# Last batch's FFN in rounds of four row groups, with Gelu taken straight from four PSUM banks

## The chip, the cores and the metric

The kernel runs on one core of a Trainium2 chip. The metric is the device time of one execution in microseconds; a kernel's time is the median of its runs. Before the change it is 4330.48 us, the median of three runs of 4320.04, 4330.48 and 4338.9 us.

## The reference

The whole computation is a two-layer network over 4 images of 384 channels and 32 x 32 positions. Layer 0 is a selective scan followed by a mixture of four experts with two chosen for each token. Layer 1 is an attention with eight heads followed by an FFN whose weights are Kronecker products. The change lies in the last of these, which is, cut to what matters:

```python
def _L1_ffn_ref(x, c_fc_1, c_fc_2, c_proj_1, c_proj_2):
    w_fc = jnp.kron(c_fc_1, c_fc_2)
    w_proj = jnp.kron(c_proj_1, c_proj_2)
    h = x @ w_fc.T
    h = jax.nn.gelu(h, approximate=False)
    out = h @ w_proj.T
    return out
...
x = x + _L1_conv_ref(_ln_c(x), L1_conv_w_qkv, L1_conv_w_out, L1_conv_b_out)
t = _to_tokens(x)
t = t + _L1_ffn_ref(_ln_t(t), L1_ffn_c_fc_1, L1_ffn_c_fc_2, L1_ffn_c_proj_1, L1_ffn_c_proj_2)
```

`w_fc` is the product of 1536 x 32 and 1 x 12 factors, `w_proj` of 32 x 1536 and 12 x 1. Because of this, the first matrix can be applied in two steps: 384 channels are reduced to 32 values (here called z), and these are multiplied by a 32 x 1536 matrix. The second matrix likewise: 1536 hidden values are reduced to 32, which are spread to 384 channels.

## The kernel before

The kernel is one program in which the four batches overlap. `scan_layer` does the selective scan of all batches, one after the other. While it scans a batch, the tail (experts, attention, FFN) of the batch before is laid beside it by a scheduler that runs a timeline of its own when the program is built and fixes the order of instructions on each engine. The tail of the last batch has no scan beside it. It runs in a wider set of buffers: `WIDE` for SBUF and, from its attention on, `WIDE_BANKS` for PSUM, which has 6 banks with the tag "p" and 2 with the tag "o", where `NARROW_BANKS` has 3 and 1.

The FFN is in `last_layers`. For each half `i` of the positions (512 of 1024 columns) a first part forms x2, the input of the FFN (L1149 to L1155, `o_ps`), its mean and variance by matmuls with ones (L1160 `x_mean`, L1177 `x_var`, with squares on ACT, L1168), and z: a matmul `z_ps` (L1171), scaled by the inverse root of the variance, which ACT works out as an Ln and an Exp (`inverse_root`, L152 and L153) and DVE multiplies in (L1180). z holds the same 32 values four times, once in each group of 32 partitions.

The second part is a loop over the two halves, with the 1536 hidden values in 12 chunks of 128, `f` = 0 to 11:

- `hidden(i, at)` makes six chunks (`ng = 6`). For each, a matmul `h_ps` (L1193) multiplies 32 rows of z by a piece of `fc1`. Chunk `f` uses the row group `f % 4` of TensorE, so that matmuls of different chunks can run in different rows of the array. They go two at a time: two banks are filled, two copies on ACT (L1199) bring them to the SBUF tile `hs`, and the next pair's first matmul is made to wait for the first copy of the pair before. Then one activation applies Gelu to the whole `hs`, 3072 columns (L1202), in place.
- Then six matmuls `f_acc` (L1210) reduce `hs` to 32 values. Chunk `f` writes to the column group `f % 4`, so these too can run beside one another, in different columns of the array. A first product and the later ones of the same column group accumulate in one bank with the tag "o".
- After two such rounds DVE copies the accumulated bank (`fy`, L1215), three matmuls `fo_ps` (L1218) spread it to 384 channels (adding up the four column groups), DVE adds x2 (L1220), and the result is stored (L1221).

Gelu and Exp need different function tables on ACT. The builder of the program puts a load of a table (ACT_TABLE_LOAD) before any activation whose function is not in the active one. `exp_again` (L145 to L148) puts a load of the table that holds both Ln and Exp directly behind a given activation, with high priority, so that the exponentials of the scan and of the attention never find a table that lacks them:

```python
self.exp_again(nc.scalar.activation(hs, hs, AF.Gelu).ins)
```

`hs` has the tag "k12", of which the wide room has three buffers. x2 holds one of them until the end, so `hs` alternates between two.

Of the kernel before, what the change touches and what calls it, by code (L numbers as in the profile page):

```python
# [11 lines left out]
AF = mybir.ActivationFunctionType  # L12
# [5 lines left out]
P = 128  # L18
# [5 lines left out]
HF = 512  # L24
# [34 lines left out]
KR = 32  # L59
# [29 lines left out]
WIDE_BANKS = {"o": 2, "p": 6}  # L89
# [26 lines left out]
class Body:  # L116
# [993 lines left out]
    def last_layers(self, b, att, room):  # L1110
# [4 lines left out]
        nc, a = self.nc, self.a  # L1115
        nq = P // KR
# [11 lines left out]
        fc1 = wc[:, 0, :].rearrange("p (q m) -> p q m", m=P)  # L1128
# [9 lines left out]
        zs = []  # L1138
        for i in range(NH):
# [4 lines left out]
            for c in range(DC):  # L1144
                ps = room.bank("p", "o_ps")
# [4 lines left out]
                for j in range(HF // P):  # L1150
                    nc.tensor.matmul(  # L1151
                        ps[:, j * P : (j + 1) * P], part[j // 2][:, j % 2, chunk], self.ident,
                        start=False, stop=(j == HF // P - 1),
# [16 lines left out]
            for c in range(DC):  # L1170
                nc.tensor.matmul(  # L1171
                    zp, wz[:, c * P : (c + 1) * P], x2[:, c, halves(i)],
                    start=(c == 0), stop=(c == DC - 1),
# [7 lines left out]
            zs.append(z)  # L1181


        ng = 6

        def hidden(i, at):
            hs = room.tile([P, ng, HF], "k12", "hs")
            early = None
            for f in range(at, at + ng, 2):
                banks = [room.bank("p", "h_ps") for _ in range(2)]  # L1190
                for o, ps in enumerate(banks):
                    rows = slice((f + o) % nq * KR, ((f + o) % nq + 1) * KR)
                    ins = nc.tensor.matmul(  # L1193
                        ps, fc1[rows, (f + o) // nq, :], zs[i][rows, :], start=True, stop=True
                    ).ins
                    if o == 0 and early is not None:
                        self.depend(ins, early)
                done = [
                    nc.scalar.copy(hs[:, f - at + o, :], ps).ins for o, ps in enumerate(banks)  # L1199
                ]  # L1200
                early = done[0]
            self.exp_again(nc.scalar.activation(hs, hs, AF.Gelu).ins)  # L1202
            return hs

        for i in range(NH):
            out = room.bank("o", "f_acc")
            for at in range(0, FC, ng):
                hs = hidden(i, at)
                for f in range(at, at + ng):
                    nc.tensor.matmul(  # L1210
                        out[f % nq * KR : (f % nq + 1) * KR, :], pj1[:, f, :], hs[:, f - at, :],
                        start=(f < nq), stop=(f >= FC - nq),
                    )
            y = room.tile([P, HF], "k4", "fy")
            nc.vector.tensor_copy(y, out)  # L1215
            for c in range(DC):
                ps = room.bank("p", "fo_ps")
                nc.tensor.matmul(ps, pj2[:, c * P : (c + 1) * P], y, start=True, stop=True)  # L1218
                o = room.tile([P, HF], "k4", "out")
                nc.vector.tensor_add(o, ps, x2[:, c, halves(i)])  # L1220
                nc.sync.dma_start(out=a["out"][b][c * P : (c + 1) * P, halves(i)], in_=o)  # L1221
# [236 lines left out]
```

## Time and profile before

The profiled execution took 4328.09 us; its span, from the first to the last instruction, is 4326.3 us.

| what | value |
|---|---|
| median of three runs | 4330.48 us |
| profiled execution, and its span | 4328.09 us, 4326.3 us |
| mean granted clock of TensorE | 0.868 of full speed |
| busy over the whole span: PE, DVE, ACT, POOL | 77%, 66%, 58%, 70% |
| last batch's FFN, 4256 to 4320 us: ACT copies (L1199) | 24, 588 ns each |
| ACT Gelu (L1202) | 4, 2762 ns each |
| ACT table loads (L1202 and L148) | 8, 1283 ns each |
| PE idle ahead of f_acc (L1210), waiting for Gelu | 20.9 us |
| ACT idle ahead of its copies, waiting for h_ps | 18.3 us |
| after the last add: flag, branch, stores landing | 4320.1 to 4326.3 us |

How to read it: the busy shares of the whole span say little about this change, since each stage has its own limits. The last 120 us of the span belong to the last batch's layer 1 alone, with PE, ACT and DVE only. In matmul rows, "128*32" is rows by columns of the array that the weights take; a matmul in fp32 is recorded as two passes, so x4 is two matmuls. A line number can be that of a helper: L152 and L153 are the Ln and Exp of `inverse_root`, L148 is the load of `exp_again`.

### The profile page before, as it was taken

The numbers are of one execution on the slowest core, as the hardware profiler recorded it, in microseconds if no ns is written. First come the engines' busy times: TensorE is split into PE (matmuls) and PEld (weight loads), VectorE is DVE, ScalarE is ACT, GpSimd is POOL, SyncE is SP. The second block draws the span as 40 slices with busy tenths as digits, with TensorE's granted clock in tenths as the row PEclk, the third lists the DMA queues.
The fourth block names the chain that finished last, engine by engine and source line by source line (L and its number), as shares of the span: only waits on it lengthen the run. The fifth ranks groups of instructions, "written<-read, shape, count | busy, mean of one in ns | idle before, by whom it ended". The sixth has DMA issues, their size and how long they took to land. (4 is left out here: it accounts for less than half of the span.)

```text
span 4326.3 us, 45583 instructions
## 1 busy us (share of the span) xinstructions
PE 3343.5 (77%) x13244; PEld 1557.7 (36%) x13244; DVE 2860.4 (66%) x4200; ACT 2517.2 (58%) x4484; POOL 3021.3 (70%) x1471
## 2 busy tenths in 40 slices
PE   6445454388997895779996887669998889999896
PEld 2111111155552222235553222216555235566322
DVE  5999997878786868678886778777887720000101
ACT  5555555456665776566764777476666654344354
POOL 5999997798898968889898689778899810000100
PEclk8666666599998997879998999769998999999997
DMA  5444564567895535558789335547889343345100
GB/s 141 129 120 129 138 166 113 178 198 228 232 278 142 138 113 167 156 157 241 220 235 269 112 100 149 160 121 210 242 227 297 99 157 105 109 141 203 50 26 19
DMA packets 410322, 693.69 MB, mean 160 GB/s; under 512 B 51024, under 2 KB 209616, under 8 KB 410064
## 3 DMA queue, kind: packets, MB, share of 16 engines
q1 hardware_dynamic: 400752, 664.29, 52.9%
q0 software_dynamic: 8192, 25.17, 1.8%
q8 instruction: 106, 1.74, 0.2%
q14 instruction: 152, 1.25, 0.1%
q10 hardware_dynamic: 1120, 1.25, 0.1%
HBM read 569.00 MB, written 121.50 MB: 160 GB/s over the span
## 5 line engine op out<-in xcount | busy, mean ns | idle before, releaser
L440 POOL TENSOR_TENSOR bx<-dtr,bcs 128x1024 f32<-128x1024 f32 x768 | 1794.6, 2364 | 202.1 <-PE acc L475 109.4
L449 ACT ACTIVATE da<-dtr,nega 128x512 f32<-128x512 f32 x1536 | 1045.1, 690 | 940.0 <-DVE bx L461 574.9
L468 POOL TENSOR_TENSOR bx<-bx,bcs 128x1024 f32<-128x1024 f32 x384 | 906.0, 2364 | 154.1 <-DVE carry L465 70.6
L475 PE MATMUL acc<-bx,sel 128*32 128x512 f32 x3072 | 501.5, 709 | 319.1 <-POOL bx L468 270.7
L927 PE MATMUL h_ps<-xc,w 128*128 128x256 f32 (+1 forms) x3168 | 664.8, 365 | 64.5 <-DMA w<-in_w 20.2
L942 PE MATMUL y_ps<-w,hs 128*128 128x384 f32 x1824 | 643.2, 505 | 46.7 <-ACT hs L935 39.8
L927 PEld LDWEIGHTS h_ps<-xc,w 128*128 128x128 f32 x3168 | 549.9, 197 | 236.8 <-issue 95.0
L454 DVE TENSOR_TENSOR_SCAN bx<-da,carry,bx 128x512 f32<-128x512 f32 x384 | 473.4, 1270 | 117.3 <-POOL bx L440 62.5
L454 DVE TENSOR_TENSOR_SCAN bx<-da,bx 128x512 f32<-128x512 f32 x384 | 452.4, 1211 | 120.1 <-ACT da L449 66.3
L454 DVE TENSOR_TENSOR_SCAN da<-da,carry,bx 128x512 f32<-128x512 f32 x384 | 476.5, 1273 | 80.0 <-ACT da L449 67.9
L461 DVE TENSOR_TENSOR bx<-da,bcs 128x512 f32<-128x512 f32 x768 | 510.5, 680 | 3.7
L454 DVE TENSOR_TENSOR_SCAN da<-da,bx 128x512 f32<-128x512 f32 x384 | 455.0, 1219 | 55.8 <-ACT da L449 44.9
L942 PEld LDWEIGHTS y_ps<-w,hs 128*128 128x128 f32 x1824 | 349.9, 196 | 334.7 <-issue 74.3
L1057 ACT ACTIVATE ex<-s_ps 128x512 f32<-128x512 f32 x512 | 299.9, 590 | 159.7 <-PE s_ps L1051 157.9
L1051 PE MATMUL s_ps<-w 64*128 64x512 f32 x1024 | 306.2, 657 | 56.7 <-ACT ex L1057 55.1
L963 POOL TENSOR_TENSOR diag<-ident,g_weight 128x1024 f32<-128x1024 f32 x8 | 15.1, 1901 | 453.9 <-PE xc_ps L910 440.7
L932 ACT ACTIVATE hs<-h_ps,bb 128x256 f32<-128x256 f32 (+1 forms) x528 | 201.1, 440 | 181.9 <-PE h_ps L927 178.1
L1097 PE MATMUL o_acc<-ex,vt 128*64 128x512 f32 x1024 | 285.9, 633 | 20.0 <-ACT ex L1057 15.7
L475 PEld LDWEIGHTS acc<-bx,sel 128*32 128x32 f32 x3072 | 76.4, 117 | 617.6 <-POOL bx L468 378.3
L946 DVE TENSOR_TENSOR y<-y_ps,bb 128x384 f32<-128x384 f32 x76 | 41.6, 548 | 236.6 <-PE y_ps L942 236.5
L365 PE MATMUL dt_ps<-xd,wdt 108*128 108x512 f32 x192 | 125.5, 741 | 85.5 <-ACT mag L404 53.3
L1051 PEld LDWEIGHTS s_ps<-w 64*128 64x128 f32 x1024 | 82.3, 188 | 255.3 <-ACT ex L1057 211.8
(217 smaller groups left out, 3605.0 us busy)
## 6 DMA issues: line engine op xcount, KB each, us to landing
w<-in_w SPq DMA_DIRECT2D x352, 576.0 KB
dtr<-dd SPq DMA_DIRECT2D x1536, 128.0 KB
bcs<-both SPq DMA_DIRECT2D x512, 128.0 KB
dd<-one_e SPq DMA_DIRECT2D x96, 256.0 KB
dd<-mag SPq DMA_DIRECT2D x96, 256.0 KB
rows<-zero SPq DMA_DIRECT2D x76, 192.0 KB
xt<-x SPq DMA_DIRECT2D x32, 384.0 KB
xs<-rows SPq DMA_DIRECT2D x32, 384.0 KB
```

The costliest lines, as they stand in the source:

```text
L440: pool = nc.gpsimd.tensor_mul(bx, dtr[q][1], bc[:, 0].unsqueeze(1).to_broadcast([P, 2, HF])).ins
L449: nc.scalar.activation(da, dtr[q][0][:, j, :], AF.Exp, scale=nega[:, col : col + 1])
L454: nc.vector.tensor_tensor_scan(run(h), run(da), run(bx[:, j, :]), 0.0 if first else hold, ALU.mult, ALU.add,)
L461: dve = nc.vector.tensor_mul(bx[:, j, :], h, cg).ins
L468: pool = nc.gpsimd.tensor_mul(bx, bx, cg.unsqueeze(1).to_broadcast([P, 2, HF])).ins
L475: nc.tensor.matmul(acc[lo : lo + DB, :], sel, out[q][:, j, :], start=(g == 0), stop=(g == NG - 1),)
L927: nc.tensor.matmul(ps[:, r, :], w1[(f + r) // wf][:, c, (f + r) % wf * P : ((f + r) % wf + 1) * P], xc[:, c, :], start=(c == 0), stop=(c = ...
L932: nc.scalar.activation(hs[:, f + r, :], ps[:, r, :], AF.Identity, bias=bb[:, f + r : f + r + 1])
L942: nc.tensor.matmul(out[:, :D], hs[:, f, t * P : (t + 1) * P], w2[f // wf][:, f % wf, :], start=(f == 0), stop=(f == FC - 1),)
L1051: ins = nc.tensor.matmul(ps, w[rows, j * P : (j + 1) * P], w[rows, halves(i)], start=True, stop=True).ins
L1057: done.append(nc.scalar.activation(ex[:, o, :], ps, AF.Exp, scale=HD**-0.5, accum_out=sums[:, t, 2 * j + o, i : i + 1],).ins)
L1097: ins = nc.tensor.matmul(out[cols, :], made[t][1][:, j, cols], ex[:, o, :], start=(j == 0), stop=(j == MB - 1),).ins
```

## The change

In the FFN of the batch that runs with `WIDE_BANKS`, that is the last one, a round is four chunks in place of six, one for each row group. A new function `quickly` takes four banks, issues the four matmuls `h_ps` one after the other with no dependency between them, and then applies Gelu to each bank on its way from PSUM to `hs`: four activations of 512 columns, in place of copies and one Gelu of 3072. It doesn't call `exp_again`. The loop over the rounds and the f_acc matmuls are as before, with `ng` of 4, so each half has three rounds. The other batches, and the exact second layer that isn't run with these inputs, keep the rounds of six.

```diff
-        ng = 6
+        alone = room.banks is WIDE_BANKS
+        ng = nq if alone else 6
+
+        def quickly(i, at):
+
+            hs = room.tile([P, ng, HF], "k12", "hs")
+            banks = [room.bank("p", "h_ps") for _ in range(nq)]
+            for o, ps in enumerate(banks):
+                rows = slice(o * KR, (o + 1) * KR)
+                nc.tensor.matmul(
+                    ps, fc1[rows, at // nq, :], zs[i][rows, :], start=True, stop=True
+                )
+            for o, ps in enumerate(banks):
+                nc.scalar.activation(hs[:, o, :], ps, AF.Gelu)
+            return hs
 
         def hidden(i, at):
+            if alone:
+                return quickly(i, at)
             hs = room.tile([P, ng, HF], "k12", "hs")
             early = None
             for f in range(at, at + ng, 2):
```

In the changed kernel the lines behind the new ones move by 16, except that `h_ps` of the last batch is L1193, its Gelu L1197, f_acc L1226, fy L1231, fo_ps L1234 and the last add L1236.

## The prediction

> **What bounds the kernel now.** I read the page first: section 2 gives POOL, ACT and DVE the first nine tenths, and section 4's chain has PE alone in the last tenth. The change touches one branch of one function, so I went to that place: the chain of waits from 4180 us on, then stretches of 3.41 us, then PE's timeline.
>
> The chain in the last batch's FFN (start, us, what):
>
> ```profile
> 4261.29 1.18 PE h_ps L1193 x8
> 4262.47 1.05 ACT hs L1199 x2
> 4263.54 1.28 ACT L1202
> 4264.84 2.77 ACT hs L1202
> 4267.65 3.47 PE f_acc L1210 x12
> ...
> 4283.68 4.92 PE fo_ps L1218 x6
> 4288.60 1.11 PE h_ps L1193 x4
> ...
> 4319.36 0.69 DVE out L1220
> ```
>
> PE and ACT take turns: matmul, copy, table load, Gelu of 3072 columns, matmul. A round of six row groups starts its f_acc 11.56 us after the one before (4267.65, 4279.21), and there are four rounds. From the end of x_var (next matmul at 4259.31 in the timeline) to the end of the last add (4320.05) the FFN takes 60.7 us, 1.4% of the span. Nothing runs beside it.
>
> The second bound is PE's clock. Stretches of 3.41 us, laid on the moments at which the granted clock changes (span; busy us of PE, PEld, DVE, ACT, POOL; clock; DMA share; GB/s):
>
> ```profile
> 2840.65:2844.07 3.42, 1.82 (x8) 0.29 (x8) 3.35 (x6) 2.98 (x6) 2.95 (x2) 1.00 0.30 100
> 2844.07:2847.48 3.41, 0.00 (x0) 0.00 (x0) 3.39 (x6) 3.38 (x5) 2.85 (x2) 1.00 0.48 156
> 2847.48:2850.89 3.41, 1.15 (x8) 0.39 (x10) 0.94 (x3) 3.39 (x2) 3.41 (x3) 0.50 0.00 0
> ```
>
> ```profile
> 4270.86:4274.28 3.42, 2.45 (x10) 0.60 (x8) 0.00 (x0) 1.35 (x3) 0.00 (x0) 1.00 0.00 0
> 4274.28:4277.69 3.41, 0.00 (x0) 0.00 (x0) 0.00 (x0) 3.38 (x4) 0.00 (x0) 0.50 0.00 0
> 4281.10:4284.52 3.42, 2.57 (x9) 0.50 (x2) 0.69 (x1) 0.00 (x0) 0.00 (x0) 0.50 0.00 0
> 4284.52:4287.93 3.41, 3.41 (x5) 1.35 (x4) 1.12 (x2) 0.00 (x0) 0.00 (x0) 0.50 0.16 62
> 4287.93:4291.34 3.41, 2.74 (x10) 0.60 (x8) 0.96 (x2) 1.07 (x2) 0.00 (x0) 1.00 0.43 169
> ```
>
> A stretch's work decides the clock of the next. The one from 2840.65 keeps full clock with PE busy 1.82 us; the one from 4270.86 loses it with 2.45 us. The former holds column-tiled matmuls that use all 128 rows (acc), the latter mostly h_ps of 32 rows. So I weigh streaming time by the share of rows in use, counting matmuls on different columns together once: the former has 1.65/3.41 = 0.48, the latter (0.19 + 4 x 0.43 x 1/2)/3.41 = 0.31. Over all 929 full-clock stretches of the trace, 0.38 separates those that keep the clock from those that lose it but for 7; over the 333 at half clock, 0.74 separates those that regain it but for 9. Weighing by rows times columns leaves 13 and 15 misfits.
>
> PE's timeline where two tilings alternate, at full clock and then at half:
>
> ```profile
> 2836.63 1.13 PE L1193 MATMUL h_ps<-z,wc 32*128 32x512 f32 x4
> 2837.69 1.05 PE L475 MATMUL acc<-bx,sel 128*32 128x512 f32 x2
> 2838.66 1.13 PE L1193 MATMUL h_ps<-z,wc 32*128 32x512 f32 x4
> ```
>
> ```profile
> 1849.57 1.94 PE L475 MATMUL acc<-bx,sel 128*32 128x512 f32 x8
> 1851.43 2.08 PE L1193 MATMUL h_ps<-z,wc 32*128 32x512 f32 x4
> 1853.44 1.94 PE L475 MATMUL acc<-bx,sel 128*32 128x512 f32 x8
> ```
>
> From start to start an h_ps turn costs 1.06 us and an acc turn 0.98; at half clock 2.01 and 1.86. The turn costs that whether it holds one matmul or four (acc x2 is one matmul in two passes, x8 is four).
>
> [...] four h_ps on four row groups took 1.14 us, no more than two; a change of mode costs about 0.1 to 0.2 us over two passes of 0.43. [...] Here the load is 1283 ns and the next activation starts 0.02 us later, [...].
>
> **The change, part by part.** The instruction order of the changed kernel is the same on POOL, SP and DVE up to the flag (and in all earlier batches).
>
> Removed: 24 copies of 0.59 us, four Gelus of 2.76, eight table loads of 1.28. On the path they were 11.56 us a round less the f_acc.
>
> Added on ACT: 24 Gelus from PSUM and four table loads. The loads don't vanish: the scheduler puts Ln and Exp of the second half's z between the first four Gelus and the rest, so ACT runs load, 4 Gelus, load, Ln, load, Exp, load, 20 Gelus. A Gelu 128x512 from PSUM isn't in this trace; nearest is Exp from PSUM (L1057, 590 ns); pitch between 0.48 (the pair of copies, 1.07 us) and 0.58 (three L1155, 1.84 us). I take 0.60 and 0.52. First load 4256.42 to 4257.70, four Gelus to 4259.92, load, Ln 0.69, load, Exp 0.63, load: 4265.1. z's product on DVE (0.69) is ready at 4264.55.
>
> Moved on PE: the order is h0-3, x_var, then f0 h4 f1 h5 f2 h6 f3 [h7 h8 h9] f4 h10 f5 h11 [f6-9] [f10 f11], fo; in the second half h0-3, h4 h5, then f and h in turn, f0 to h11, [f6-9] [f10 f11], fo. So f and h, which before ran two or four at once, now mostly run alone: that is the price. First half from 4259.31: 6 f turns x 0.98 + 6 h turns x 1.06 = 12.2, the last six f 0.12 + 4 x 0.43 = 1.83: 4273.4. Then 0.2 to the end of the accumulation, fy 0.70, and fo at 4274.35. That needs full clock: an f and an h turn weigh (0.85 + 0.85/4)/2.03 = 0.52, above 0.38, so it holds. fo at full clock is 6 x 0.43 + 0.1 to 0.2 = 2.75 (4.92 before): 4277.1. Second half: h0-3 and h4 h5 2.0, 12.2, 1.83 = 16.1: 4293.2; accumulation, fy, three fo and the last add 4.7: 4297.9. Before: 4320.05. **Gain 22.2 us.**
>
> What hides ACT: the fifth Gelu ends at 4265.7 and f4's turn comes at 4267.4; h9 needs z at 4266.4, there at 4264.55. In the second half Gelu needs 0.52 for a PE pair of 2.03. [...] Reused hs buffers wait for f turns already past. The banks of h4 and h5 in the second half wait for the adds of fo, 0.7 us after fo, as now. On the other side, turns that overlapped would gain up to 10 us.
>
> The profiled execution is 4328.09 us, with span 4326.3; the median shown is 4330.48, 2.4 above. Before's tail also depends on where the 3.41 us grid falls: moving it over the same schedule made before's end 0 to 6 us later (mean 3), while the changed one, at full clock throughout, does not move. I take 24.5 off the median: **4306 us**.
>
> **The rivals.**
> - Area counts, not rows: lone f and h turns weigh a quarter, the clock falls at about 4264 and again in the second half. Then first half: 4281.8; fo at half clock to 4287.5; second half seven turns at full clock and seven at half: end 4318.4, gain 1.7, **4329 us**. For it: the misfits are few either way. Against: the stretches shown. If only the first half falls, 4319.
> - Slower: full clock is lost before f0 of each half and can't come back, as (1.71 + 0.43)/3.87 = 0.55 is under 0.74. Then 6 x 1.86 + 6 x 2.01 + 3.4 = 26.6 a half; end 4328.7, **8.6 later, 4339 us**. It decides if a stretch under 0.38 lies at the start of a half; the h0-5 there run four at once and follow dense matmuls, which speaks against it.
> - More: f and h overlap or turns are shorter, ACT's Gelus bind: about 8 us less, **4298 us**.
> - "Not reloaded" is not what happens (four loads remain); costed above.
>
> **How the numbers follow.** Forecast 0.72 (own range 4299 to 4314, since the runs before spread over 19 us), area 0.12, slower 0.06, more 0.10. 0.5% is 21.7 us, a line at 4308.8 and 4352 for what can be told from no change here: the forecast lies just past it, so I put 0.60 of its 0.72 beyond. Faster 0.60 + 0.10 = 0.70; slower by over 0.5% only if half clock meets the upper end of the spread of the runs, 0.03; same 0.27. Range 4294 to 4322: [...].
>
> **What would show it.** PEclk 1.00 from 4256 us to the end; f_acc alone per turn at 0.98, h_ps 1.06; four table loads after 4256 us; the last add about 22 us earlier; ACT waiting for h_ps, not PE for Gelu. Wrong if the clock reads 0.50 within the f and h turns, if turns take 1.9 us, or if PE waits for Gelu over 4 us.

## The result, and the profile after

The changed kernel takes 4311.09 us (median of 16 runs, 4303.55 to 4330.8) against 4330.12 us of the kernel before (16 runs on the same chip, 4317.05 to 4345.93). The ratio is 0.9957, with a 95% interval of 0.9944 to 0.9971: 19 us less, between 12.6 and 24.2. The forecast was 4306 us, in a range of 4294 to 4322.

The single runs of one kernel spread over 27 to 29 us, so a stage of 60 us is better measured inside the traces. The measure used below is **the tail: from the start of the first x_var matmul of the last batch's second half to the end of the last add**. It was 4255.28 to 4320.05 before, 64.77 us, and is 4258.63 to 4301.93 now, 43.30 us: 21.5 us less. Each tail below comes from one trace; the kernel before, traced twice, gave 64.77 and 64.67 us.

The two profiled executions differ by less, 4328.09 - 4310.15 = 17.9 us. The part ahead of the tail, in which the order of instructions is the same, took 3.35 us longer in the profile after, and what follows the last add 0.2 us longer.

The chain of waits of the changed kernel (start, us, what):

```profile
4258.63 1.12 PE x_var L1177 x2
...
4262.74 0.98 PE f_acc L1226 x2
4263.71 1.05 PE h_ps L1193 x2
4264.76 0.98 PE f_acc L1226 x2
...
4274.91 1.89 PE f_acc L1226 x12
...
4277.63 2.84 PE fo_ps L1234 x6
4280.47 1.91 PE h_ps L1193 x10
4282.38 0.04 issue
4282.41 1.12 PE h_ps L1193 x2
4283.53 0.98 PE f_acc L1226 x2
...
4301.24 0.69 DVE out L1236
```

ACT has left the chain. PE alone carries it: one f_acc, one h_ps, one f_acc, at 0.98 and 1.05 us a turn, and fo_ps at full clock in 2.84 us where it took 4.92. The first fo_ps starts 19.00 us after the tail's start.

ACT's timeline of the changed kernel (start, us, line, operation; in brackets the idle time ahead and what ended it):

```profile
4263.16 1.28 ACT L152 ACT_TABLE_LOAD   x1
4264.46 0.69 ACT L152 ACTIVATE z<-x_var,eps 128x512 f32<-128x512 f32 x1
4265.16 1.28 ACT L153 ACT_TABLE_LOAD   x1
4266.45 0.63 ACT L153 ACTIVATE z<-z 128x512 f32<-128x512 f32 x1
4267.10 1.28 ACT L1197 ACT_TABLE_LOAD   x1
4268.40 1.58 ACT L1197 ACTIVATE hs<-h_ps 128x512 f32<-128x512 f32 x3
...
4274.95 0.60 ACT L1197 ACTIVATE hs<-h_ps 128x512 f32<-128x512 f32 x1 [1.43 <-PE h_ps L1193]
```

Three of the four loads are seen here, and each is followed within 0.02 us of its end by the next activation. A lone Gelu from a bank takes 0.60 us, and ACT waits for h_ps ahead of it.

A stretch of 3.41 us in the second half (busy us of PE, PEld, DVE, ACT, POOL; clock; DMA share; GB/s):

```profile
4284.45:4287.86 3.41, 3.41 (x8) 0.85 (x8) 0.00 (x0) 1.04 (x3) 0.00 (x0) 1.00 0.00 0
```

The clock is 1.00 in it, and in every stretch of the tail.

One thing wasn't foreseen. DVE's timeline between the halves:

```profile
4278.79 0.69 DVE L1236 TENSOR_TENSOR out<-fo_ps,x 128x512 f32<-128x512 f32 x1 [1.22 <-PE fo_ps L1234]
4279.65 0.69 DVE L1236 TENSOR_TENSOR out<-fo_ps,x 128x512 f32<-128x512 f32 x1 [0.17 <-PE fo_ps L1234]
4281.67 0.69 DVE L1236 TENSOR_TENSOR out<-fo_ps,x 128x512 f32<-128x512 f32 x1 [1.33 <-PE h_ps L1193]
```

The third add stands still for 1.33 us, although its bank was full at 4280.47, and h5, the sixth h_ps of the second half (4282.41 in the chain), waits for the bank that it frees. The trace names PE h_ps as the releaser, but the add reads nothing of h_ps. The instruction just ahead of it on DVE waits for two semaphores and is recorded at 4281.57. One of the two is raised by the store of the first result; that store was issued at 4279.51, and its last update of the semaphore is recorded at 4281.55. An experiment below (fy_kw) takes this wait away.

### The profile page after: what moved, and what is told of

It reads as the page before. It is cut to its first block, busy times and chain, and to the rows that moved or that the text cites. A ratio compares the mean times of both kernels' runs of the same rounds, so it can differ in the third digit from the quotient of the medians.

```text
span 4308.4 us, 45575 instructions
## 1 busy us (share of the span) xinstructions
PE 3340.9 (78%) x13244; PEld 1561.4 (36%) x13244; DVE 2853.4 (66%) x4200; ACT 2501.4 (58%) x4476; POOL 3019.4 (70%) x1471
## 3 DMA queue, kind: packets, MB, share of 16 engines
q8 instruction: 106, 1.74, 0.2%
## 5 line engine op out<-in xcount | busy, mean ns | idle before, releaser
L1097 PE MATMUL o_acc<-ex,vt 128*64 128x512 f32 x1024 | 284.8, 631 | 20.3 <-ACT ex L1057 16.6
```

Source lines behind the costliest of these rows:

```text
L1097: ins = nc.tensor.matmul(out[cols, :], made[t][1][:, j, cols], ex[:, o, :], start=(j == 0), stop=(j == MB - 1),).ins
```

## The experiments

The runs came in three groups, each beside the kernel before on the same chip, so ratios are to that. All tails are from traces. lone_h, below, leaves work out and isn't listed; fy_kw, lone_h and before_again were run once.

| kernel | tail, us | ratio to before, 95% |
|---|---|---|
| before; before_again | 64.77; 64.67 | 1 |
| noreload (before, without reloads) | 57.20 | 0.9988 (0.9976 to 1.0001) |
| copies4 (after, with copies and one Gelu) | 50.61 | 0.9964 (0.9950 to 0.9977) |
| reload (after, with reloads) | 43.83 | 0.9949 (0.9930 to 0.9967) |
| **after** | 43.30 | 0.9957 (0.9944 to 0.9971) |
| six_direct (after, rounds of six) | 42.34 | 0.9936 (0.9917 to 0.9954) |
| fy_kw (after, fy elsewhere) | 42.09 | single run |
| ahead2 | 34.74 | 0.9922 (0.9903 to 0.9941) |
| ahead | 33.58 | 0.9928 (0.9908 to 0.9947) |
| f_together | 32.46 | 0.9927 (0.9906 to 0.9948) |
| ahead2_ln | 31.94 | 0.9934 (0.9915 to 0.9953) |
| ahead_ln | 31.43 | 0.9930 (0.9916 to 0.9944) |

**Undo "not reloaded": reload.**

```diff
             for o, ps in enumerate(banks):
-                nc.scalar.activation(hs[:, o, :], ps, AF.Gelu)
+                ins = nc.scalar.activation(hs[:, o, :], ps, AF.Gelu).ins
+            self.exp_again(ins)
```

> The table of exponentials is loaded again behind the last Gelu of each round: about 12 table loads of 1.28 us in the tail instead of 4, all else as in the changed kernel. Theory A (ACT has slack: about 4.7 us of work a round with both loads against about 8.2 us of PE turns, and a Gelu's result is needed several turns later): the stretch from the first x_var matmul to the end of the last add stays within 1 us of 43.3 us. Rival B (the loads stand on the path, as in the kernel before, where the PE waited for ACT): 8 loads x 1.28 = 10 us longer, 53 us, and 4321 us in all.

The tail is 43.83 us, 0.5 us more, with 12 loads. ACT's timeline:

```profile
4253.40 1.28 ACT L148 ACT_TABLE_LOAD   x1
4254.69 1.28 ACT L1197 ACT_TABLE_LOAD   x1
4255.98 2.06 ACT L1197 ACTIVATE hs<-h_ps 128x512 f32<-128x512 f32 x4
```

At the end of the first half, where the changed kernel does its last Gelus one at a time with up to 1.43 us of idling ahead of them, two loads stand here and then four Gelus in a row. PE waits for them once, in the last six f_acc, which take 2.34 us in the chain where the changed kernel's took 1.89:

```profile
4256.82 2.34 PE f_acc L1227 x12
```

That is nearly all of the 0.5 us. Theory A: ACT has slack, and in the changed kernel's order eight loads cost 0.5 us of the 10.3 that they last.

**That part alone, in the kernel before: noreload.**

```diff
-            self.exp_again(nc.scalar.activation(hs, hs, AF.Gelu).ins)
+            ins = nc.scalar.activation(hs, hs, AF.Gelu).ins
+            if room.banks is not WIDE_BANKS:
+                self.exp_again(ins)
```

> The kernel before with one part of the change alone: the table of exponentials is not loaded again behind the Gelus of the last batch; rounds of six, copies and one Gelu over 128x3072 stay. Theory A (of the loads only that ahead of a Gelu stands on the path, since the one behind it runs while PE does f_acc; the first one remains): 3 x 1.28 = 3.8 us less, the stretch from the first x_var matmul to the end of the last add is 61 us instead of 64.8. Rival B (every load stands on the path): 7 x 1.28 = 9.0 us, 56 us. Rival C (PE alone is the bound): 64.8 us.

The tail is 57.20 us, 7.6 less, between A and B. Its chain:

```profile
4290.64 3.46 PE f_acc L1212 x12
...
4294.93 2.84 PE fo_ps L1220 x6
...
4301.29 1.18 PE h_ps L1193 x8
4302.47 1.06 ACT hs L1199 x2
4303.53 0.02 issue
4303.55 2.77 ACT hs L1202
```

From the copies ACT goes straight to Gelu: three loads are gone from the chain, 3.8 us, as A has it. The rest is in fo_ps: some 2.85 us twice, not 4.92. The clock came back in time for both, 2 x 2.08 = 4.2 us. PE's timeline of the f_acc ahead of the first fo_ps, in noreload and then in the kernel before:

```profile
4290.64 3.44 PE L1212 MATMUL f_acc<-hs,wc 128*32 128x512 f32 x12 [3.95 <-ACT hs L1202]
4279.21 3.63 PE L1210 MATMUL f_acc<-hs,wc 128*32 128x512 f32 x12 [5.23 <-ACT hs L1202]
```

PE's wait is shorter by a load. The f_acc then fell almost wholly into one stretch, from 4290.34 to 4293.75, and the next stretch had full clock; before, a border at 4281.10 split them, and the two stretches behind that border ran at half clock (0.50 each, with PE busy for 2.57 and 3.41 us). That the place on the grid makes this difference is read from these traces and was not tried by itself. Together that is 8.0; some 0.4 were lost in h_ps that ran partly at half clock. So removing loads is worth 7.6 us in one order of work (seven loads) and 0.5 in the other (eight), and more than half of the 7.6 is clock. The whole kernel's time doesn't show it: the interval of noreload's ratio, 0.9976 to 1.0001, takes in no change.

**Undo "Gelu from the banks": copies4.**

```diff
-                nc.scalar.activation(hs[:, o, :], ps, AF.Gelu)
+                nc.scalar.copy(hs[:, o, :], ps)
+            nc.scalar.activation(hs, hs, AF.Gelu)
```

> Rounds of four and no reload, but the four banks are copied out and one Gelu goes over 128x2048, as in the kernel before. Theory A (reading the banks is worth what it takes out of the chain h, copy, Gelu, f): ACT needs 4 x 0.49 + 1.9 = 3.9 us a round instead of 2.1, and becomes the bound of the second half; 3 to 7 us longer than 43.3 us in the stretch from the first x_var matmul to the last add, 4314 to 4318 us in all. Rival B (the rounds of four and the missing loads alone make the gain): within 1 us of 43.3 us. Rival C (PE rests so long between its groups that the clock falls to half): 12 us or more longer, mean clock of the tail under 0.8.

The tail is 50.61 us, 7.3 more, just above A's 3 to 7. The chain of its second half:

```profile
4272.68 1.94 ACT hs L1197 x4
4274.62 0.02 issue
4274.64 1.91 ACT hs L1198
4276.55 1.94 ACT hs L1197 x4
4278.50 0.02 issue
4278.52 1.92 ACT hs L1198
4280.44 0.04 issue
4280.48 1.98 PE f_acc L1227 x8
...
4283.23 5.31 PE fo_ps L1235 x6
```

ACT is the bound, as A says, at 3.9 us a round. C is there as well: the last f_acc and the fo_ps of both halves run at half clock, the mean clock of the tail is 0.70, and the two fo_ps alone take 5.49 + 5.31 - 2 x 2.85 = 5.1 us more. Its sizing (12 us or more) was too large, since ACT covers part of the slow matmuls. B is refuted.

**Undo "rounds of four": six_direct.**

```diff
-        ng = nq if alone else 6
+        ng = 6
...
-            banks = [room.bank("p", "h_ps") for _ in range(nq)]
+            banks = [room.bank("p", "h_ps") for _ in range(ng)]
...
-                rows = slice(o * KR, (o + 1) * KR)
+                rows = slice((at + o) % nq * KR, ((at + o) % nq + 1) * KR)
...
```

> Rounds of six row groups instead of four, Gelu still straight from six banks and no reload of the table. Theory A (the size of the round matters little, because h_ps and f_acc interleave one by one anyway and as many turns of PE remain): the stretch from the first x_var matmul to the end of the last add is within 1.5 us of the 43.3 us of the changed kernel, clock 1.00. Rival B (four at once on the four row groups is what makes the gain): at least 4 us longer, 47 us or more.

The tail is 42.34 us, 1.0 less than with rounds of four, and the clock stays at 1.00, as A has it. The 1.0 us lies ahead of the first fo_ps, which starts 18.03 us after the tail's start instead of 19.00; the third add waits here too, for 1.34 us. The rounds of four bring nothing where Gelu reads banks: in both kernels f_acc and h_ps mostly go one by one.

**The third add's wait: fy_kw.**

```diff
-            y = room.tile([P, HF], "k4", "fy")
+            y = room.tile([P, HF], "kw" if alone else "k4", "fy")
```

> For the last batch the tile fy lies in another buffer ring, so that the third add of the first half no longer takes the buffer of the first result, whose store is still under way. Theory A (this add waited for the store to land, 1.33 us, and h_ps number five of the second half behind it): the third add follows the second after 0.17 us, one h turn of about 1.1 us goes, the stretch from the first x_var matmul to the last add is 42.2 us. Rival B (the add waits for PE h_ps, as the releaser in the timeline says): the idle time of 1.33 us stays and the stretch is 43.3 us.

The tail is 42.09 us, 1.2 less. DVE's timeline:

```profile
4280.51 1.49 DVE L1236 TENSOR_TENSOR out<-fo_ps,x 128x512 f32<-128x512 f32 x2 [1.27 <-PE fo_ps L1234]
4282.16 0.69 DVE L1236 TENSOR_TENSOR out<-fo_ps,x 128x512 f32<-128x512 f32 x1 [0.17 <-PE fo_ps L1234]
```

The third add follows at once, and the chain has h_ps x12 in 1.92 us at 4282.13 in place of x10, a pause and x2. So the add waited for its buffer, and that for a store to land, whose last semaphore update came 2.04 us after its issue (256 KB, issued by SP; in the kernel before, from 4286.52 to 4288.53, 2.01 us). What these 2 us consist of is not shown.

**What decides the clock: lone_h.**

```diff
-                rows = slice(o * KR, (o + 1) * KR)
+                rows = slice(0, KR)
...
+                    if alone and f < FC - nq:
+                        continue
```

> All h_ps matmuls of the last batch use row group 0 (the same 32 rows of weights, so other values of h), and the first eight f_acc matmuls of each half are left out: 12 h_ps matmuls in a row, each alone on 32 of 128 rows. Rule A (a stretch of 3.41 us keeps full clock by its streaming time times the share of rows in use, at least about 0.38): weight 0.25, the clock falls to 0.50 in the second half's run of h_ps and their pitch goes from 0.85 to 1.7 us. Rule B (busy time alone counts): PE is busy nearly all of the time, the clock stays 1.00 and each takes 0.85 us.

Its stretches, with the same columns as above:

```profile
4251.39:4254.80 3.41, 3.41 (x9) 1.41 (x8) 0.00 (x0) 2.84 (x6) 0.00 (x0) 1.00 0.00 0
4258.22:4261.63 3.41, 3.41 (x6) 1.32 (x5) 0.69 (x1) 3.37 (x5) 0.00 (x0) 0.50 0.00 0
```

and the chain, where x24 is twelve matmuls:

```profile
4279.42 18.08 PE h_ps L1193 x24
```

PE was busy for all of the first stretch and the clock fell at its end. By rows in use, an estimate from its timeline, it weighs (6 x 0.43 x 1/4 + 0.62 of x_var)/3.41 = 0.37, just under the 0.38 fitted to the trace before. At half clock PE was busy all the time through five stretches, 4254.80 to 4271.87, and the clock stayed down; the twelve matmuls of the second half took 1.51 us each on average, and the last eight of the first half, all at half clock, 1.74 (13.95 us in all). Rule B is refuted. The stretch of the changed kernel shown in the result has the same PE busy time of 3.41 us, but an f_acc turn and a part of a second on 128 rows in it, and keeps full clock. It weighs 0.44 to 0.47, according to where in an overlapping record the streaming is put; counted so, the two stretches at which lone_h lost full clock (from 4251.39 and 4278.69) come to 0.34 to 0.39, so the margin is small. All these weights are estimates. Weighing by area is refuted by the two together: it gives the changed kernel's stretch 0.2, which kept full clock, and lone_h's first 0.34 to 0.37, which lost it.

**Fewer turns: f_together.**

```diff
...
+                    if alone and f == at:
+                        self.depend(ins, self.last)
```

Here `ins` is the round's first f_acc and `self.last` the round's last Gelu.

> The first f_acc matmul of each round of the last batch waits for the round's last Gelu, so that the four f_acc of a round run together on their four column groups instead of one by one between h_ps matmuls. Theory A (the tail is bounded by the number of PE turns, h turns of 1.06 us and f turns of 0.98 us): fewer turns, the stretch from the first x_var matmul to the end of the last add shortens from 43.3 us by 2 to 4 us, and the clock stays at 1.00. Rival B (the Gelus' own pace or the wait for them decides, 0.5 us a piece, six times four of them): 0 to +3 us. Time against the changed kernel: 4307 to 4309 us under A, 4311 to 4314 under B.

The tail is 32.46 us, 10.8 less: A in direction, far above its size. The clock did not stay at 1.00, as A had it: one stretch, from 4250.03, ran at half. The chain of the second half:

```profile
4257.40 3.90 PE h_ps L1193 x16
4261.30 1.00 PE f_acc L1226 x8
4262.29 1.11 PE h_ps L1193 x6
4263.40 1.56 ACT hs L1197 x3
4264.96 0.04 issue
4265.01 1.11 PE f_acc L1226 x8
```

Four f_acc now share one turn of 1.00 us. From the end of fo_ps to the start of fy the second half takes 8.7 us instead of 17.1; the first half, to fo_ps, 16.6 instead of 19.0. What the expectation didn't price is that the h_ps pile up behind the Gelus and then share turns too: three take 1.11 us in the chain above. Two things stand beside the turns. The third add of the first half follows the second after 0.17 us here, so the wait that fy_kw prices at 1.2 us is gone as well. And ACT's pace begins to count, as B has it, though the tail doesn't grow: nine Gelus run on end from 4258.55 to 4263.06, and the last f_acc wait for the three behind them.

**Beyond: ahead, ahead_ln, ahead2, ahead2_ln.** In f_together ACT idles 6.75 us between the halves. These kernels issue each round's h_ps ahead of the f_acc of the round before; "_ln" moves Ln and Exp of the second half's z ahead of the first Gelu; "2" puts the first half's fo_ps behind more h_ps.

```diff
+            for n, (i, at) in enumerate(rounds):
+                now, last = hs, self.last
+                if n + 1 < len(rounds):
+                    hs = quickly(*rounds[n + 1])
+                fold(outs[i], at, now, last)
+                if at == FC - ng:
+                    finish(i, outs[i])
...
+                if i == at == 0:
+                    self.depend(self.last, self.root)
```

`fold` is the loop over f_acc, `finish` the part from fy to the store, `self.root` the second half's Exp. The last addition is the "_ln" part.

> As f_together (f_acc in fours behind the round's last Gelu), and each round's h_ps is put ahead of the f_acc of the round before it, over the border between the halves too. Theory A (with the turns grouped, ACT becomes the bound, and it idled 6.75 us between the halves of f_together): Gelus run on at 0.50 us from one half into the next, the stretch from the first x_var matmul to the last add falls from 32.5 to about 26 us. Rival B (PE now has too little streaming to keep the clock): half clock in two or more stretches of 3.41 us, 28 to 31 us. Rival C (h_ps of the second half cannot go ahead because the six banks are full): 32 us, no change.

> As ahead, and Ln and Exp of the second half's z come before the first Gelu, so that one table load remains of four. Theory A (ACT is the bound of the tail, the three loads of 1.28 us stand on its chain, and waiting for x_var gives part back): x_var 4.1 + Ln and Exp 1.3 + load 1.3 + 24 Gelus at 0.51 + f 1.0 + fy 0.7 + fo 2.8 + add 0.7 = about 24 us. Rival B (PE rests some 3 us at the beginning and the clock falls to half for the f_acc and fo behind it): 27 us or more, no better than ahead.

> As ahead_ln, and the fo_ps of the first half and its adds come behind the h_ps of the second half's second round, so that ACT has Gelus to do meanwhile. Theory A (ACT's idle time of 5.0 us between the halves, with fo_ps in it, is the largest wait left in the tail): the stretch from the first x_var matmul to the end of the last add falls from 31.4 to about 27 us. Rival B (fo_ps needs banks that the h_ps hold, and its adds then hold the next h_ps up; or the clock falls in more stretches): 30 us or more.

> As ahead2_ln, but with Ln and Exp of the second half's z between the first four Gelus and the rest, with four table loads. Theory A (ACT bounds the whole tail): three loads more at 1.28 us, of which ahead showed 2.2 us on the path: about 29 us. Rival B (PE or the clock bounds it): within 0.7 us of ahead2_ln.

The tails are 33.58, 31.43, 31.94 and 34.74 us. ahead came out near its rival C's time, 1.1 us worse than f_together: only one round of h_ps went across the border, ACT still idled 5.1 us there, and half clock came in three stretches, as B has it. Whether full banks held the h_ps back was not tried. ahead_ln is 2.2 us better than ahead, but not the 24 us of its theory A. ahead2_ln went by its rival B: the idle time between the halves shrank to 3.3 us, but two stretches ran at half clock instead of one, and the tail is 0.5 us longer. ahead2 is 2.8 us behind ahead2_ln, near A's difference, but 1.5 us of that is its last fo_ps, 4.32 us partly at half clock where ahead2_ln's took 2.86; how much the loads themselves cost isn't shown. In all of these the clock was at half for one to four stretches, and none came below 31 us. PE idled ahead of an h_ps (2.68 us in ahead, 1.45 in ahead_ln and ahead2_ln), where the changed kernel's chain has 0.04 us at most ahead of its h_ps.

The five versions with grouped f_acc have ratios of 0.9922 to 0.9934, with overlapping intervals: which is best isn't settled. ahead_ln has the shortest tail and the narrowest interval, which meets that of the change at its end (0.9916 to 0.9944 against 0.9944 to 0.9971); the chips differ.

**The grid's place: before_again.**

> The kernel before once more, for the place of its tail on the grid of 3.41 us. Theory A (the time of the tail depends on where the grid falls, 0 to 6 us above the profile shown, 3 us in the mean): a stretch from the first x_var matmul to the end of the last add of 65 to 71 us, with other stretches at half clock. Rival B (it depends little on it): within 1 us of 64.8 us.

The tail is 64.67 us, as B says. But this is a weaker test than meant: the grid lay at 1.78 us of 3.41 from the tail's start, and at 1.90 in the first profile. Over all 14 profiles it lies between 1.76 and 3.06, ten of them between 1.76 and 2.02. Whether another place would lengthen the tail was therefore not tried; such places didn't come up.

## Why the prediction was right, and where it was off

- **The direction and the mechanism were right.** The forecast for the tail was a gain of 22.2 us (4320.05 - 4297.9); the traces show 21.5. That it is so close is partly luck, since two misses below cancel in part.
- **The prices of the turns were right**: 1.06 and 0.98 us forecast, 1.05 and 0.98 measured. The first fo_ps was forecast 4274.35 - 4255.28 = 19.07 us after the tail's start, and came after 19.00. fo_ps: 2.75 forecast, 2.84 measured.
- **The clock was right**: 1.00 throughout. Rows in use, the estimate behind the forecast, fits lone_h (0.37, clock lost) and the changed kernel (0.44 to 0.47, clock kept) together, where busy time (3.41 us in both) and area (0.34 to 0.37 lost, 0.2 kept) don't. Over all stretches of the trace before, some 930 at full clock and some 330 at half, with the prediction's thresholds and the 0.43 us put at the start of each record, it leaves 8 misfits and 8, near the prediction's 7 and 9. The best threshold for plain busy time leaves 17 and 13, so this count alone says little, and the estimate rests on the two runs. Of the rivals, area fell with the stretch at 1.00, and half clock throughout with it.
- **ACT was hidden, as said**: reload, with eight loads more, costs 0.5 us, and an activation starts within 0.02 us of the end of the load ahead of it.
- **The step that was mis-sized: "The banks of h4 and h5 in the second half wait for the adds of fo, 0.7 us after fo, as now."** Not as now. Before, fo_ps at half clock spread the adds apart:

```profile
4285.80 0.69 DVE L1220 TENSOR_TENSOR out<-fo_ps,x 128x512 f32<-128x512 f32 x1 [2.17 <-PE fo_ps L1218]
4287.50 0.69 DVE L1220 TENSOR_TENSOR out<-fo_ps,x 128x512 f32<-128x512 f32 x1 [1.02 <-PE fo_ps L1218]
4288.65 0.69 DVE L1220 TENSOR_TENSOR out<-fo_ps,x 128x512 f32<-128x512 f32 x1 [0.46 <-PE fo_ps L1218]
```

  So the first result's store had landed (last update at 4288.53) when the third bank was full (4288.60), by 0.07 us. At full clock the first two adds are 0.86 us apart, the third waits 1.33 us for the store, and h5 needs a turn of its own: h0 to h5 took 3.06 us, where the prediction has 2.0. fy_kw prices it at 1.2 us, more than the whole gap between forecast and tail (0.7 us). The other terms were together some 0.5 us too high, most of it in the 4.7 us put on what follows the second half's last f_acc, which took 4.34.
- **The term for the grid, 2.3 us on top of 22.2, is an estimate that has no support in the runs.** It rests on places of the grid spread evenly, and 14 profiles show that they aren't; what another place would do wasn't tried. The total of 24.5 us lies just outside the measured 12.6 to 24.2, while the tail's 21.5 lies inside.
- **The 5 us between 4306 and 4311.09** are thus 2.3 of the grid term, 0.7 of the tail, and about 2 that the tail doesn't explain. Those 2 us are less than the interval leaves open, some 6 us to either side. In profiles with one and the same order of work the part ahead of the tail varied by more: 4256.41 us in ahead, 4281.89 in ahead_ln, on one chip. Its cause wasn't looked for.
- **"More", the rival in which turns overlap and some 8 us more go, was no description of this kernel but of the next**: the turns can be shared, if f_acc is made to wait for its round (10.8 us, of which up to 1.2 may be the third add's wait).

What each part of the change was worth depends on the others. Without the reloads, but with the old order, 7.6 of the 21.5 us are there (noreload). Rounds of four, with copies and without reloads, reach 14.2 (copies4). Gelu from the banks brings the rest, and with it the reloads and the size of the round hardly matter (reload, six_direct).

## What to carry to other kernels

Count PE's turns, not its matmuls: a tiled matmul that goes alone costs as much here as four side by side (1.05 us against 1.07 for h_ps), so it may pay to make the first of a group wait for the last of its inputs. Before removing an engine's idle time, weigh what the stretch leaves on PE, by rows in use (an estimate, from 0.37 and 0.44 to 0.47 above). A shorter wait went with a clock that came back in noreload, where fo_ps took 2.84 us instead of 4.92, and 1.45 us of idle time of PE with one that was lost in ahead2_ln, where an h_ps turn of four took 2.02 us and an f_acc turn 1.87, instead of 1.07 and 1.00. And where a stage gets faster, look at buffers whose stores used to have time to land: here 0.07 us to spare before, a wait of 1.33 us after.

## What the runs showed of the hardware

- The clock fell after a stretch in which PE was busy for 3.41 of 3.41 us, mostly with 32-row matmuls (lone_h, from 4251.39; weight 0.37), and stayed at 1.00 after one as busy with 128-row matmuls among them (the changed kernel, from 4284.45; 0.44 to 0.47). Between these two, busy time doesn't decide; the weights are estimates from their timelines.
- In the traces of the kernel before and the changed one, the granted clock changes in steps of 3.41 us: 224 and 210 spans of one clock lie between the first span and the last, and each is a multiple of 3.413 us within 0.004 us. This grid didn't lie at random to the program: 1.76 to 3.06 us after the tail's start in 14 profiles, within 0.26 us of each other in ten of them, though the tail's start itself varied from 4238.00 to 4281.89 us over chips and runs. Why was not tried.
- A wait on two semaphores was put down to an engine with no part in it (PE h_ps), where it was a store's landing, 2.04 us after its issue.
- Eight more table loads of 1.28 us cost 0.5 us in a place where ACT idled up to 1.43 us ahead of a Gelu.
